# Last stage: three column groups in work in a turn, transposes a step ahead, TensorE in program order

## The chip, the cores and the metric

The kernel runs on one core of a Trainium2 chip. The metric is the time of one execution on that core in microseconds (us). TensorE (PE in the profile) does matrix products and transposes and writes to PSUM; PEld is its weight loading; VectorE is DVE, ScalarE is ACT, GpSimd is POOL, SyncE is SP. Everything here is float32.

## What is computed

Two layers follow each other on an image x of 4 x 64 x 256 x 256. The change touches only the end of the second layer: attention along columns, and the feed-forward network after it. Cut to that, the reference is (E = 64 channels, 4 heads, one query and one key number per head):

```python
h = h + _lin_attn(_ln(h.swapaxes(1, 2), cn_g, cn_b), col_wq, ..., col_bo).swapaxes(1, 2)
f = _ln(h, fn_g, fn_b)
f = gelu(f @ w1.T + b1) @ w2.T + b2          # 64 -> 256 -> 64
return moveaxis(h + f, -1, 1)                # back to channels first

def _lin_attn(x, ...):                       # per column, over its 256 rows
    q = elu(x @ wq.T + bq) + 1;  k = elu(x @ wk.T + bk) + 1;  v = x @ wv.T + bv
    q = q / mean(q);  k = k / sum(k)
    return (q @ (k.T @ v)) @ wo.T + bo
```

## The kernel before

The kernel is a chain of stages with DRAM tensors between them. `stage_d`, the last, reads `hd` (the image after the row attention, rows outermost, 64 channels innermost) and writes the output. Its unit is a **column group**: one image b and 32 columns, so 4 x 8 = 32 groups. A group's tile `h` holds 128 x 32 x 2 x 64 numbers: partition = row within a half, then column, row half, channel (16 KB a partition). `load` fetches it with four DMAs from SP's queue.

A group passes through two generators, which the loop at the end of the stage advances in alternation with `_steps`, one piece of each per round:

- `attn` takes the sums of the layer norm (`spread`, four times 128 x 1024 elements: sum, centring, square, sum of squares), transposes `h` in eight steps of four 128 x 128 blocks (L1203), copies each result out of PSUM on ScalarE (L1205), and forms the query and key numbers (L1212). After the last step it scales them (`rstd`, L1219, L1220), puts them through elu (`feature`, L695 and L696) and has `f` and `kz` (L1229, L1232). Then comes a serial part: key-value sums (L1238, L1242), a transpose (L1245, L1259), `mix` (L702 to L710), and the result, added to `h` in place (L1271 and L1274 on TensorE, L1277 on VectorE). At last the layer norm of the new `h` (`spread`, `rstd`) fills the tiles `xf` (L1288), of which there are five.
- `ffn` takes the previous group in eight steps. In each step r it turns `xf` (four transposes at L1298, copied to `xfT` at L1300), multiplies by w1 (four products of 64 rows each, L1311; each pair uses the two halves of the array's rows) with Gelu on ScalarE (L1313), and then gathers in one PSUM bank the transposed `h` (L1319) plus the products with w2 (four, 64 columns wide, L1322). VectorE adds the bias and writes to the output tile `st` (L1324). The transposes of step r + 1 stand behind the w1 products of step r.

So two groups are in work in a turn of the loop: attention of group n, feed-forward of group n - 1, and 33 turns in all. Group n is loaded one turn ahead; three `h` tiles exist. Two groups share one `st` of 128 x 128 x 64, and after every second group eight DMAs from POOL's queue write it to the output: 512 KB each, in runs of 64 columns (256 bytes).

PSUM has eight banks: six for tiles called `mm`, two for `sm`. Every product above of 512 columns takes one `mm`.

What sets the order on an engine is a planner: it takes the instructions as the program issues them, and orders each engine's own list by readiness in its model of time, earlier-issued ones first. So in this kernel an engine's list is not the program's order, TensorE's included; each engine then runs its list strictly in order, waiting where an operand or a buffer isn't ready.

Of the kernel before, what the change touches and what calls it, by code (L numbers as in the profile page):

```python
# [249 lines left out]
def kernel(ctx: ExitStack, tc: tile.TileContext, x, packs, fd, out, off):  # L250
# [888 lines left out]
    def stage_d():  # L1139
        with ExitStack() as cs:  # L1140
# [27 lines left out]
            def load(b, g):  # L1168
                h = p.tile([128, 32, 2, C], F32, name="h", bufs=3)
                for rh in (0, 1):  # L1170
                    for j in (0, 1):
                        SY.dma_start(h[:, 16 * j:16 * j + 16, rh, :], hd[b, rh * 128:(rh + 1) * 128, :, 2 * g + j, :])
                return h

            def spread(src, n, s2):

                s1 = p.tile([128, n], F32, tag="ln_s", name="ln_s")
                V.tensor_reduce(s1, src, AX.X, ALU.add)  # L1178
                xc = p.tile([128, n, C], F32, tag="xc", name="xc")
                V.scalar_tensor_tensor(xc, bc(s1, C), -LN_S, src, ALU.mult, ALU.add)  # L1180
                sq = p.tile([128, n, C], F32, tag="ln_sq", name="ln_sq")
                S.activation(sq, xc, AF.Square)  # L1182
                V.tensor_reduce(s2, sq, AX.X, ALU.add)  # L1183
                return xc

            def rstd(s2, n):
                s3 = p.tile([128, n], F32, tag="ln_d", name="ln_d")
                S.activation(s3, s2, AF.Sqrt, bias=eps_t, scale=LN_S)
# [4 lines left out]
            def attn(h, xfs):  # L1193

                qp = p1.tile([128, 32, 32], F32, name="qp")
                v1 = p1.tile([128, 64], F32, name="v1")
                for r in range(8):
                    if r % 2 == 0:
                        k = r // 2
                        spread(h[:, 8 * k:8 * k + 8].rearrange("p c a e -> p (c a) e"), 16, v1[:, 16 * k:16 * k + 16])  # L1200
# [5 lines left out]
                    yield  # L1206
                    if r % 4 == 0:
                        qk = sm()
# [5 lines left out]
                    if r % 4 == 3:  # L1214

                        V.transpose(qp[:, r // 4 * 16:r // 4 * 16 + 16].rearrange("p c m -> p (c m)"), qk)
# [4 lines left out]
                yield  # L1221
# [8 lines left out]
                fv = f.rearrange("p r k c h -> p r k (c h)")  # L1230
                kz = p1.tile([128, 2, 128], F32, name="kz")
                V.tensor_tensor(kz.rearrange("p r (c h) -> p r c h", h=4), f[:, :, 1], rs.rearrange("p (c r) -> p r c", r=2).unsqueeze(3).to_broadcast([128, 2, 32, 4]), ALU.mult)  # L1232
                yield

                t = mm()
                for rh in (0, 1):
                    for g in range(4):
                        T.matmul(t[g * 32:(g + 1) * 32, :], kz[:, rh, g * 32:(g + 1) * 32], h[:, 8 * g:8 * g + 8, rh, :], start=(rh == 0), stop=(rh == 1))  # L1238
                qs = sm()
# [39 lines left out]
                for hf in (0, 1):  # L1279
                    v2 = p.tile([128, 32], F32, name="v2")  # L1280
                    xcs = []
                    for k in (2 * hf, 2 * hf + 1):
                        xcs.append(spread(h[:, 8 * k:8 * k + 8].rearrange("p c a e -> p (c a) e"), 16, v2[:, (k % 2) * 16:(k % 2) * 16 + 16]))
                        yield
                    rs = rstd(v2, 32)
                    for k in (0, 1):
                        xf = p.tile([128, 8, 2, C], F32, name="xf", bufs=5)
                        V.tensor_tensor(xf.rearrange("p c a e -> p (c a) e"), xcs[k], bc(rs[:, k * 16:k * 16 + 16], C), ALU.mult)  # L1288
                        xfs.append(xf)

            def ffn(h, xfs, st, gi):


                def first(r):
                    t = mm()
                    xf = xfs[r // 2]
                    for i in range(4):
                        T.transpose(t[:, i * 128:(i + 1) * 128], xf[:, (r % 2) * 4 + i].rearrange("p a e -> p (a e)"), ident)  # L1298
                    xT = p.tile([128, 512], F32, name="xfT")
                    S.copy(xT, t)  # L1300
                    return xT

                yield
# [66 lines left out]
```

## Time and profile before

| | us |
|---|---|
| median of three runs | 8939.46 (8939.42 to 8940.79) |
| the profiled execution | 8937.15 |
| its span, first to last instruction | 8935.4 |
| within it: the stage's first transpose of `h` (L1203) | 6690.1 |
| first w1 product (L1311) | 6742.5 |
| first w1 product of the last turn | 8863.2 |
| last write to `st` ends | 8908.3 |

The span less than the time by 1.75 us is launch and end. The stage has its start (52.4 us), 31 like turns ((8863.2 - 6742.5) / 31 = 68.4 us each), a last turn with the feed-forward network alone (45.1 us), and the output's last DMAs (27.1 us): 2245.3 us, a quarter of the span. Whole-kernel shares (PE 92%, DVE 66%, ACT 51%, POOL 13%) are means over stages with other limits, and say little of this one; a stretch of one turn is to be read on its own. DMAs take 29% of the 16 engines' time in this stage: 15.3% are the output's, 14.1% the loads of `h`.

### The profile page before, as it was taken

The page shows a single profiled execution, that of the slowest core. Times are in us where ns is not written, and L with a number is a line of the kernel's source. Part 1 is how long each engine was busy: PE and PEld are TensorE (multiplying, and loading weights), DVE is VectorE, ACT ScalarE, POOL GpSimd, SP SyncE. Part 2 cuts the span into 40 slices and gives each one's busy share as a digit, 9 for nine tenths or more (in the row PEclk, how much of TensorE's full clock was granted, in tenths as well). Part 3 has the DMA queues.
Part 4 walks back from the last instruction along what each step waited for, and adds up shares of the span by engine and source line. Part 5 has one row for each costly group of instructions (what it writes and reads, how often), then busy time and mean ns, then how long its engine had stood idle before and what let it go on. Part 6 is the DMA issues. An engine that isn't in the chain of part 4 may idle for free. (4 is left out here: it accounts for less than half of the span.)

```text
span 8935.4 us, 143218 instructions
## 1 busy us (share of the span) xinstructions
PE 8237.0 (92%) x57518; PEld 4221.3 (47%) x57518; DVE 5940.4 (66%) x8506; ACT 4587.6 (51%) x7782; POOL 1133.1 (13%) x1828
## 2 busy tenths in 40 slices
PE   8999999699999998999999999999988888989897
PEld 6777777344444443333333344444443333333333
DVE  7766666377777773222222488888877888788776
ACT  4455554455555552222222366666656677667765
POOL 1111111112222221000000011111110000000000
PEclk9999999799999999999999999999998999999998
DMA  7777777799999998888888755555542233233232
GB/s 164 160 187 184 183 185 176 219 357 390 392 390 389 394 378 304 299 296 297 298 298 295 240 170 170 170 170 170 169 121 45 54 70 67 48 76 65 50 67 48
DMA packets 1258502, 1832.48 MB, mean 205 GB/s; under 512 B 335600, under 2 KB 1040112, under 8 KB 1196656
## 3 DMA queue, kind: packets, MB, share of 16 engines
q1 hardware_dynamic: 1053296, 1034.63, 38.5%
q0 software_dynamic: 204544, 788.69, 27.0%
q8 instruction: 456, 7.47, 0.3%
q14 instruction: 206, 1.69, 0.1%
HBM read 967.65 MB, written 788.53 MB: 197 GB/s over the span
## 5 line engine op out<-in xcount | busy, mean ns | idle before, releaser
L915 DVE TENSOR_TENSOR y<-ge,mm 128x512 f32<-128x512 f32 (+1 forms) x640 | 406.0, 634 | 1211.8 <-ACT ge L914 1211.8
L882 PE MATMUL mm<-t,w 128*128 128x512 f32 (+1 forms) x2560 | 1093.7, 566 | 19.1 <-DMA t<-td 19.1
L914 ACT ACTIVATE ge<-mm 128x512 f32<-128x512 f32 (+1 forms) x640 | 354.7, 554 | 1253.8 <-PE mm L889 1253.8
L1313 ACT ACTIVATE hg<-mm,b 128x512 f32<-128x512 f32 x1024 | 631.7, 685 | 331.0 <-PE mm L1311 328.7
L775 PE MATMUL mm<-gp,wc 128*64 128x510 f32 (+1 forms) x3072 | 702.4, 596 | 89.0 <-DVE xm L785 51.0
L620 PEld LDWEIGHTS mm<-wqk,gp 128*128 128x128 f32 x6144 | 728.0, 197 | 99.0 <-issue 60.7
L620 PE MATMUL mm<-wqk,gp 128*128 128x128 f32 x6144 | 761.5, 282 | 1.1 <-POOL gp L589 0.9
L882 PEld LDWEIGHTS mm<-t,w 128*128 128x128 f32 x2560 | 455.2, 189 | 647.5 <-issue 436.9
L1322 PE MATMUL mm<-hg,pack_d 128*64 128x512 f32 x2048 | 579.8, 609 | 101.0 <-ACT hg L1313 101.0
L1311 PE MATMUL mm<-xfT,w 64*128 64x512 f32 x2048 | 637.7, 665 | 2.9 <-ACT xfT L1300 2.2
L830 ACT COPY tb<-mm 128x512 f32<-128x512 f32 x512 | 300.1, 587 | 631.3 <-PE mm L824 631.2
L889 PE MATMUL mm<-t,w 64*64 64x504 f32 (+1 forms) x5120 | 575.6, 555 | 0.0
L824 PE MATMUL mm<-xl,pack_c 64*128 64x512 f32 x2048 | 511.7, 601 | 6.0 <-ACT xl L812 4.6
L775 PEld LDWEIGHTS mm<-gp,wc 128*64 128x64 f32 x3072 | 277.9, 137 | 468.8 <-issue 330.8
L316 ACT ACTIVATE ln_sq<-xn 128x1024 f32<-128x1024 f32 x256 | 274.2, 1071 | 365.9 <-DVE xn L314 365.8
L318 DVE TENSOR_REDUCE ln_v<-ln_sq 128x16 f32<-128x1024 f32 x256 | 312.0, 1219 | 184.2 <-ACT ln_sq L316 184.1
L1324 DVE TENSOR_SCALAR st<-mm,pack_d 128x512 f32<-128x512 f32 x256 | 279.2, 1090 | 171.8 <-PE mm L1322 171.8
L970 PE MATMUL mm<-ya,pack_e 128*64 128x512 f32 x1024 | 381.7, 616 | 11.4 <-DMA ya<-yd 11.4
L1182 ACT ACTIVATE ln_sq<-xc 128x1024 f32<-128x1024 f32 x256 | 266.9, 1055 | 219.8 <-DVE xc L1180 219.7
L828 DVE COPY tb<-mm 128x512 f32<-128x512 f32 x512 | 344.8, 685 | 23.7 <-PE mm L824 18.2
L1311 PEld LDWEIGHTS mm<-xfT,w 64*128 64x128 f32 x2048 | 220.5, 202 | 271.5 <-issue 159.4
L889 PEld LDWEIGHTS mm<-t,w 64*64 64x64 f32 x5120 | 158.1, 132 | 374.4 <-issue 374.4
(458 smaller groups left out, 15178.4 us busy)
## 6 DMA issues: line engine op xcount, KB each, us to landing
t<-td SPq DMA_DIRECT2D x256, 1152.0 KB, 10.0
td<-tb POOLq DMA_DIRECT2D x144, 1024.0 KB, 16.1
td<-tb POOLq DMA_DIRECT2D x288, 512.0 KB, 13.9
yd<-y POOLq DMA_DIRECT2D x128, 1152.0 KB, 10.1
ya<-yd SPq DMA_DIRECT2D x192, 512.0 KB, 5.7
xs<-in_x_dram SPq DMA_DIRECT2D x128, 512.0 KB, 6.8
projd<-pj POOLq DMA_DIRECT2D x256, 256.0 KB, 6.1
gp<-projd SPq DMA_DIRECT2D x128, 512.0 KB, 9.3
```

Of the source, the lines that this page charges most:

```text
L620: T.matmul(qp[:, k * 128:(k + 1) * 128], gp[:, 2 * i + k // 2, at + dx:at + dx + 128], wqk[:, dx, :], start=(dx == 0), stop=(dx == 2))
L775: T.matmul(tv[i * 64:(i + 1) * 64, :, o], wc[2 * pr + i][:, dx, :], gps[i][:, 2 * r:2 * r + 2, i_], start=(dx == 1), stop=False, skip_grou ...
L824: T.matmul(t, inT[q, hf * 128:(hf + 1) * 128], xls[b // 2, s][q, :, 2 * y:2 * y + 2].rearrange("p f y t -> p f (y t)"), start=True, stop=True)
L828: V.tensor_copy(o, i_)
L882: T.matmul(t[:, :n], w[:, 0:128], x_[:, c, :], start=True, stop=False, skip_group_check=True)
L889: T.matmul(t[po:po + 64, :n].rearrange("p (n c) -> p n c", c=64)[:, :, o], w[q:q + 64, 128:192], x_[q:q + 64, c, i_], start=False, stop=Tr ...
L914: S.activation(ge[:, :n], ts[0][k][:, :n], AF.Gelu)
L915: V.tensor_tensor(y[:, c, :].rearrange("p n c -> p (n c)"), ge[:, :n], ts[1][k][:, :n], ALU.mult)
L970: T.matmul(t[b * 64:(b + 1) * 64, :], owT, ya[:, :, 2 * r:2 * r + 2, b * 64:(b + 1) * 64].rearrange("p f y t -> p y f t"), start=True, sto ...
L1311: T.matmul(t, w1[rh * 64:(rh + 1) * 64, i * 128:(i + 1) * 128], xT[rh * 64:(rh + 1) * 64], start=True, stop=True)
L1313: S.activation(g, t, AF.Gelu, bias=b1[:, i:i + 1])
L1322: T.matmul(y[rh * 64:(rh + 1) * 64, :], w2[:, i, :], hg[i * 2 + rh], start=False, stop=(i == 1), skip_group_check=True)
```

## The change

- **Three groups.** `attn` is cut in two. `scores(n + 1)` does the sums, transposes and query/key numbers up to `f` and `kz`; `result(n)` does the serial part, the addition to `h`, and `xf`. The feed-forward network of group n - 1 runs beside both. A group so takes three turns, and the loop 34. `h` is loaded two turns ahead, into four tiles; `xf` has six.
- **Transposes a step ahead.** The network is cut in three functions. In step i of a turn the program issues the transposes of step i + 2 (`turn`), the w1 products and Gelus of step i + 1 (`first`), a piece of `scores` and a piece of `result`, then the residual and w2 products of step i (`second`), and again a piece of each. This runs on across the border between groups: step i counts over all groups.
- **Order.** All of it stands in a block in which TensorE's instructions are issued in the program's order. The other engines keep the planner.
- `spread` takes two blocks in one call: both sums, centrings and squares first, then both sums of squares. `scores` issues its four blocks in two such calls.
- `st` becomes 128 x 128 x 32, one for each group, with four DMAs of 512 KB for each; runs of 32 columns (128 bytes).

The arithmetic is the same. The diff, with most of the removed lines cut (the functions before stand above):

```diff
@@ -1166,59 +1166,86 @@
...
             def load(b, g):
-                h = p.tile([128, 32, 2, C], F32, name="h", bufs=3)
+                h = p.tile([128, 32, 2, C], F32, name="h", bufs=4)
                 for rh in (0, 1):
                     for j in (0, 1):
                         SY.dma_start(h[:, 16 * j:16 * j + 16, rh, :], hd[b, rh * 128:(rh + 1) * 128, :, 2 * g + j, :])
                 return h
 
...
+            def spread(h, ks, v):
+                xcs, sqs = [], []
+                for k in ks:
+                    src = h[:, 8 * k:8 * k + 8].rearrange("p c a e -> p (c a) e")
+                    s1 = p.tile([128, 16], F32, tag="ln_s", name="ln_s")
+                    V.tensor_reduce(s1, src, AX.X, ALU.add)
+                    xc = p.tile([128, 16, C], F32, tag="xc", name="xc")
+                    V.scalar_tensor_tensor(xc, bc(s1, C), -LN_S, src, ALU.mult, ALU.add)
+                    sq = p.tile([128, 16, C], F32, tag="ln_sq", name="ln_sq")
+                    S.activation(sq, xc, AF.Square)
+                    xcs.append(xc)
+                    sqs.append(sq)
+                for i, k in enumerate(ks):
+                    V.tensor_reduce(v[:, 16 * i:16 * i + 16], sqs[i], AX.X, ALU.add)
+                return xcs
...
-            def attn(h, xfs):
+            def scores(n):
+                h = hs[n]
                 qp = p1.tile([128, 32, 32], F32, name="qp")
                 v1 = p1.tile([128, 64], F32, name="v1")
...
+                def up(r):
                     t = mm()
                     for i in range(4):
                         T.transpose(t[:, i * 128:(i + 1) * 128], h[:, r * 4 + i].rearrange("p a e -> p (a e)"), ident)
                     xT = p.tile([128, 512], F32, name="xT")
                     S.copy(xT, t)
...
+                    return xT
+                def score(r, xT, qk):
...
                     for g in range(4):
                         T.matmul(qk[g * 32:(g + 1) * 32, r % 4 * 128:r % 4 * 128 + 128], cwt, xT.rearrange("p (c n) -> p c n", c=4)[:, :, g * 32:(g + 1) * 32],
                                  start=True, stop=True)
...
+                def back(k, qk):
+                    V.transpose(qp[:, k * 16:k * 16 + 16].rearrange("p c m -> p (c m)"), qk)
+                xT = up(0)
+                spread(h, (0, 1), v1[:, 0:32])
+                yield
+                yield
+                qk = sm()
+                for r in range(7):
+                    if r == 4:
+                        back(0, qk)
+                        qk = sm()
+                    score(r, xT, qk)
+                    xT = up(r + 1)
+                    yield
+                    if r < 5:
+                        if r == 4:
+                            spread(h, (2, 3), v1[:, 32:64])
+                        yield
+                score(7, xT, qk)
+                back(1, qk)
                 rs = rstd(v1, 64)
...
-                yield
...
@@ -1227,15 +1254,20 @@
...
-                fv = f.rearrange("p r k c h -> p r k (c h)")
                 kz = p1.tile([128, 2, 128], F32, name="kz")
                 V.tensor_tensor(kz.rearrange("p r (c h) -> p r c h", h=4), f[:, :, 1], rs.rearrange("p (c r) -> p r c", r=2).unsqueeze(3).to_broadcast([128, 2, 32, 4]), ALU.mult)
+                fks[n] = f, kz
+            def result(n):
+                h = hs[n]
+                f, kz = fks.pop(n)
                 yield
 
...
+                fv = f.rearrange("p r k c h -> p r k (c h)")
...
@@ -1278,73 +1310,82 @@
                     yield
                 for hf in (0, 1):
                     v2 = p.tile([128, 32], F32, name="v2")
-                    xcs = []
-                    for k in (2 * hf, 2 * hf + 1):
-                        xcs.append(spread(h[:, 8 * k:8 * k + 8].rearrange("p c a e -> p (c a) e"), 16, v2[:, (k % 2) * 16:(k % 2) * 16 + 16]))
-                        yield
+                    xcs = spread(h, (2 * hf, 2 * hf + 1), v2)
+                    yield
                     rs = rstd(v2, 32)
                     for k in (0, 1):
-                        xf = p.tile([128, 8, 2, C], F32, name="xf", bufs=5)
+                        xf = p.tile([128, 8, 2, C], F32, name="xf", bufs=6)
                         V.tensor_tensor(xf.rearrange("p c a e -> p (c a) e"), xcs[k], bc(rs[:, k * 16:k * 16 + 16], C), ALU.mult)
-                        xfs.append(xf)
...
+                        xfs[n, 2 * hf + k] = xf
                     yield
...
+            def turn(i):
+                n, r = divmod(i, 8)
+                t = mm()
+                xf = xfs[n, r // 2]
+                for k in range(4):
+                    T.transpose(t[:, k * 128:(k + 1) * 128], xf[:, (r % 2) * 4 + k].rearrange("p a e -> p (a e)"), ident)
+                xT = p.tile([128, 512], F32, name="xfT")
+                S.copy(xT, t)
+                xTs[i] = xT
+            def first(i):
+                xT = xTs.pop(i)
+                hgs[i] = []
+                for k in (0, 1):
+                    for rh in (0, 1):
+                        t = mm()
+                        T.matmul(t, w1[rh * 64:(rh + 1) * 64, k * 128:(k + 1) * 128], xT[rh * 64:(rh + 1) * 64], start=True, stop=True)
+                        g = p.tile([128, 512], F32, tag=f"hg{rh}{k}", name=f"hg{rh}{k}")
+                        S.activation(g, t, AF.Gelu, bias=b1[:, k:k + 1])
+                        hgs[i].append(g)
+            def second(i):
+                n, r = divmod(i, 8)
+                h, hg = hs[n], hgs.pop(i)
+                if r == 0:
+                    sts[n] = p.tile([128, 128, 32], F32, name="st")
+                st = sts[n]
+                y = mm()
+                for k in range(4):
+                    T.matmul(y[:, k * 128:(k + 1) * 128], h[:, r * 4 + k].rearrange("p a e -> p (a e)"), ident, is_transpose=True, start=(k == 0), stop=False, skip_group_check=True)
+                for k in (0, 1):
+                    for rh in (0, 1):
+                        T.matmul(y[rh * 64:(rh + 1) * 64, :], w2[:, k, :], hg[k * 2 + rh], start=False, stop=(k == 1), skip_group_check=True)
+                V.tensor_scalar(st[:, :, 4 * r:4 * r + 4].rearrange("p r c -> p c r"), y.rearrange("p (c r) -> p c r", c=4), K("b2"), None, ALU.add)
+                if r == 7:
+                    b, g = seq[n]
+                    for q in (0, 1):
                         for rh in (0, 1):
...
+                            y0 = rh * 128 + q * 64
+                            G.dma_start(out[b, :, y0:y0 + 64, g * 32:g * 32 + 32], sts[n][rh * 64:(rh + 1) * 64, q * 64:(q + 1) * 64])
+                    del hs[n]
 
             seq = [(b, g) for b in range(B) for g in range(8)]
...
+            N = len(seq)
+            hs, fks, xfs, xTs, hgs, sts = {}, {}, {}, {}, {}, {}
+            hs[0] = load(*seq[0])
+            with tc.manual_schedule(engines={mybir.EngineType.PE}):
+                for n in range(-1, N + 1):
+                    if 0 <= n + 2 < N:
+                        hs[n + 2] = load(*seq[n + 2])
+                    gs = scores(n + 1) if n + 1 < N else iter(())
+                    gr = result(n) if 0 <= n < N else iter(())
+                    for r in range(8):
+                        i = 8 * (n - 1) + r
+                        if 0 <= i + 2 < 8 * N:
+                            turn(i + 2)
+                        if 0 <= i + 1 < 8 * N:
+                            first(i + 1)
+                        next(gs, 0)
+                        next(gr, 0)
+                        if 0 <= i < 8 * N:
+                            second(i)
+                        next(gs, 0)
+                        next(gr, 0)
+                    _steps(gs, gr)
 
     stage_d()
 
```

## The prediction

> **What bounds it now.** I first cut the stage into turns by the repeats of the L1311 group and asked for the busy times of one turn (columns: stretch, length, then busy time and instructions of each engine, granted TensorE clock, DMA share, GB/s):
>
> ```profile
> 7221.44:7289.72 68.28, 60.87 (x350) 26.64 (x350) 54.53 (x68) 47.38 (x70) 2.57 (x4) 0.97 0.15 34
> ```
>
> No engine is full: TensorE 60.87 us (89%), VectorE 54.53 (80%), ScalarE 47.38. So I read TensorE's timeline of that turn, with what ended each wait:
>
> ```profile
> 7221.44 3.39 PE L1311 MATMUL mm<-xfT,w 64*128 64x512 f32 x8 [0.18 <-ACT xfT L1300]
> ...
> 7229.50 1.98 PE L1311 MATMUL mm<-xfT,w 64*128 64x512 f32 x6
> 7231.41 0.42 PE L1212 MATMUL sm<-xT,cwt 128*32 128x128 f32 x8
> 7231.77 1.12 PE L1311 MATMUL mm<-xfT,w 64*128 64x512 f32 x2
> ...
> 7247.70 1.07 PE L1322 MATMUL mm<-hg,pack_d 128*64 128x512 f32 x2
> 7250.32 2.23 PE L1322 MATMUL mm<-hg,pack_d 128*64 128x512 f32 x6 [1.55 <-ACT hg L1313]
> ...
> 7279.91 2.81 PE L1322 MATMUL mm<-hg,pack_d 128*64 128x512 f32 x8 [1.63 <-ACT hg L1313]
> ...
> 7288.33 0.66 PE L1298 MATMUL mm<-pack_k,xf 128*128 128x128 f32 x4 [3.32 <-DVE xf L1288]
> ```
>
> Three things are to be seen. The border between groups costs a wait of 3.32 us for `xf`, which VectorE has only just made. Gelus come late for L1322 twice. And after the border's wait the eight L1311 instructions take 3.39 us; elsewhere they take 1.92. Also, where the planner put L1212 inside a set of L1311 (7229.50 to 7232.82), the set took 1.91 + 1.05 us: a pair that would use both row halves was broken up. The waits that the timeline names in this turn sum to 3.32 + 1.63 + 1.55 + 0.37 + 0.32 + 0.18 + 0.17 = 7.5 us.
>
> The last turn has only the network, undisturbed, and shows what a step costs:
>
> ```profile
> 8878.43 1.99 PE L1311 MATMUL mm<-xfT,w 64*128 64x512 f32 x8
> 8880.35 0.66 PE L1298 MATMUL mm<-pack_k,xf 128*128 128x128 f32 x4
> 8880.84 0.60 PE L1319 MATMUL mm<-pack_k,h 128*128 128x128 f32 x4
> 8881.37 1.94 PE L1322 MATMUL mm<-hg,pack_d 128*64 128x512 f32 x8
> 8883.24 1.99 PE L1311 MATMUL mm<-xfT,w 64*128 64x512 f32 x8
> ```
>
> From start to start that is 1.92 + 0.49 + 0.53 + 1.87 = 4.81 us. By starts in the same way, `scores` costs 0.59 (L1203) + 0.36 (L1212) = 0.95 a step, and `result` 1.85 (L1238) + 0.92 (L1242) + 0.25 (L1245) + 0.26 (L1259) + 0.43 (L702) + 3.90 (L1271, L1274, twice) = 7.6 a turn. TensorE's own work in a turn: 8 x 4.81 + 8 x 0.95 + 7.6 = **53.7 us**. A turn is 68.3, so 14.6 us are lost: 7.5 in waits, and some 7 in slow or broken sets (border 1.5, two broken pairs 2.1, late Gelus 1.4 and 0.9, the rest small).
>
> Here a rule is to be weighed. Read as a floor, the row's 60.87 us of busy PE would leave at most 7.4 us a turn, and with the waits below (7.2) nothing at all. The Trainium skill (Perfetto Trace Analysis, Identifying the Most-Contended Engine) says that matmul occupancy is a bad measure of distance from the roofline, and to read weight loading as well: 26.64 / 68.28 = 39%. I go by the starts, 53.7, since the undisturbed step shows it at work.
>
> **The change, part by part.**
>
> *Transposes a step ahead, across the border.* `xf` of the next group is made at r = 3 and 4 of a turn and first turned at r = 6, two steps (over 11 us) later. The 3.32 us wait goes, with it the slow set after it (1.5 us). Gelus get a whole step instead of half of one before L1322 wants them, which covers a table load, square-root work and table load back (1.28 + 0.35 + 1.28 = 2.9 us between Gelus): the 1.55 and 1.63 go, and their drawn-out sets.
>
> *Program order.* The four products of `first` stand together, so no pair is broken: -2.1 us. All removals together lead to the 53.7. In exchange TensorE can no longer take other ready work when it must wait. Three places do:
>
> 1. `kz`. The last L1212 of a group is followed, before L1238 wants `kz`, by `second` (2.40), `turn` (0.49), `first` (1.92), `up` (0.59) and `second` (2.40): 7.8 us. Before, VectorE's rows from there run
>
> ```profile
> 7246.59 0.71 DVE L1216 STREAM_TRANSPOSE qp<-sm 128x512 f32<-128x512 f32 x1
> ...
> 7248.30 0.55 DVE L1190 RECIPROCAL ln_r<-ln_d 128x64 f32<-128x64 f32 x1 [1.01 <-ACT ln_d L1188]
> ...
> 7254.81 0.42 DVE L1232 TENSOR_TENSOR kz<-f,ln_r 128x256 f32<-128x256 f32 x1
> ```
>
> and L1212 had ended at 7244.8, so `kz` came 10.4 us after it. 10.4 - 7.8 = 2.6 us of wait. Behind L1238 stand L1242, L1245 and all of the next step, and ScalarE's Gelus wait for those. Ends: 0 (the chain's own operations sum to about 6) and 11 (rival below); I take 2.6, the row's latency.
>
> 2. The two L1271 blocks take four of the six `mm` banks at once. The first stands about 1 us behind `first`, whose four Gelus take 2.4 us: 1.4 us of wait. The second needs the four additions of the first (2.48 us, L1277) and stands a `second` (2.40) behind it, plus the `st` write of 1.09: 1.2. Sum 2.6; ends 0 (before, these rows show no wait named) and 5.
>
> 3. VectorE's load is uneven. At r = 3 it has 2 x (1.21 + 1.22 + 1.20) = 7.26 for `spread`, 1.09 for `st`, 0.35 and 2.36 for `xf`: 11.1 us, and r = 4 the same, while TensorE has 4.81 + 0.95 = 5.8. With six banks TensorE gets about a step ahead of the `st` writes, not more. Ends: 0, if VectorE does `scores`' sums early, in r = 1 and 2 (3.3 and 6.1 us of its work against 6.5 and 9.7 of TensorE's; `h` has landed a turn before), and 10.6, if `st` stands behind both `spread`s. I take 2, nearer the low end, because VectorE in the turn before does run `spread` in its free places.
>
> 53.7 + 2.6 + 2.6 + 2 = **61 us a turn** (60.9).
>
> *Three groups, four `h`.* The same instructions per group, so no busy time is added. SP's four loads of a group are issued a turn earlier; they take 5.4 us to land and now have a turn and more. If that cover were gone they would cost the 5.4 once per group; SP has nothing else in its queue.
>
> *Activation tables.* Still three square roots and one exponential a group between Gelus, 8 loads of 1.28 us; one or two may merge or be added (±2.6 us of ScalarE, which has 47.4 of 61): nothing.
>
> *`st`, one per group.* L1324 takes 1.09 us with an inner stride of 256 bytes, L1277 of the same size 0.68; the stride becomes 128. Ends: -3.3 us a turn of VectorE and 0; I take 0. POOL issues four DMAs a group as before, 1.10 us each for 2048 runs; 4096 runs may take 2.2, 8.8 us a turn on an engine that has 2.6 busy. The only other POOL work, the memset of `zn`, is done a turn early.
>
> The runs are halved to 128 bytes. Row: at the end eight DMAs with 8 x 2048 runs of 256 bytes take 23.5 us, 27.1 from the last `st` write to the end of the span. Four DMAs with 4096 runs are as many runs. By the run that stays 27.1; by the byte it is 15. The Trainium skill (DMA: Bandwidth & Descriptors, Specifications) speaks against it: under 512 bytes the DMA does a read-modify-write. If that doubled a run's time, the end would be near 50. But 256 bytes are under 512 already, so the row holds that price: I take 25. In a turn the output's share was 15.3%; by the run it becomes 34% of 61 us, with the loads' 16% half of the DMA engines' time, hidden behind the turn. Without that cover (a st tile comes round after two turns) it would cost what exceeds a turn, and there is none.
>
> **The sum.** Start: `scores` of group 0 alone until `kz`, 6690.1 to 6711.2 = 21 us, then a turn of `result(0)` with `scores(1)`; `result` alone took 41 (to 6752.2), and VectorE's second load makes it 47: 68, where 52.4 were. Then 30 turns of 61 = 1830; one without `scores`, 61 - 7.6 and a little less VectorE: 52; the last, 8 x 4.81 = 38.5; end 25. Together 2013.5 against 2245.3: -232 us. 8937.15 - 232 = **8705**. The profiled execution stands 2.3 us under the median, well inside what is uncertain here.
>
> **Rivals.**
>
> - *VectorE becomes the bound.* Its 54.5 us of a turn, plus about 2.5 of the serial part that nothing fills (before: waits for L1274, L1238, L702 of 3.3 + 2.1 + 1.9): 57 us a turn. 68 + 1710 + 48 + 38.5 + 25 = 1889.5: **8581**. For it: 54.5 and 53.7 are nearly equal. Against it: it asks 95% of an engine that runs in list order.
> - *PSUM and ScalarE hold TensorE oftener.* Every step takes seven `mm` of six; at r = 7 ScalarE has Gelus, square root, exponential and three table loads, 7.8 us against TensorE's 5.2. With item 3 at half its upper end (5.3), and 1 and 2 at 6 together: 65 us. 68 + 1950 + 56 + 38.5 + 25 = 2137.5: **8829**.
> - *Slower: steps in lockstep.* If each `st` write stands behind all of its step's `spread`, TensorE in program order waits in each step for the slowest engine: 10.6 + 6.5 + 9.7 + 11.1 + 11.1 + 9.1 + 6.7 + 7.8 = 72.6 us a turn, total 2373, **9065**. It decides from 68.5 us a turn (where 31 turns and the longer start eat all). For it: nothing else can fill TensorE's waits now. Against it: `spread`'s inputs are ready early, and the list is planned with TensorE's order known.
> - *Nothing told apart*, turns between 68 and 69: the 14.6 us lost are replaced by as many.
>
> **Chances.** Forecast (59 to 63 us a turn, 8643 to 8767) 50%; VectorE's bound 15%; PSUM and ScalarE (63 to 68) 25%; lockstep 7%; nothing 3%. Under 0.2%, 18 us, a measurement of this kernel hardly tells a change. So faster 90%, same 3%, slower 7%. The range goes to 8590, which leaves out half of the VectorE case, and to 8850, which leaves out lockstep, nothing, and the top of the third case.
>
> **What would show it.** Right: turns of about 61 us between the first L1311 of each eighth step; L1298 without a wait for `xf`; L1311 always x8 in 1.92; granted clock near 1.00 in the stage; waits at L1238 for `kz` of some 2.6 us. Wrong: waits at L1311 or L1319 for the bank of a `st` write or a Gelu of more than 5 us a turn (third or lockstep case); VectorE over 92% busy (first rival); an end after the last `st` write well over 27 us (the runs). The forecast falls if L1238's wait is over 5 us, or the start over 90.

## The result, and the profile after

The changed kernel takes 8836.58 us (median of 4 runs, 8829.69 to 8839.12). Its ratio to the kernel before is 0.9885, with a 95% interval of 0.9867 to 0.9902: faster, by some 100 us where 232 were forecast. The time lies inside the range on record (8590 to 8850), but near its upper end. The profiled execution took 8839.12 us, with a span of 8837.3, and is compared here with the profiled 8937.15 of before.

The forecast was a sum over pieces of the stage. The same pieces, cut in the trace of after:

| piece | forecast, us | trace of after, us | from where to where |
|---|---|---|---|
| start | 68 | 71.3 | 6688.05 to 6759.34, the first transposes of turn 1 |
| 30 turns | 1830 | 1968.4 | to 8727.74 |
| turn without `scores` | 52 | 53.3 | to 8781.00 |
| last turn | 38.5 | 37.8 | to 8818.79, the last `st` write |
| end | 25 | 18.5 | to 8837.3 |
| sum | 2013.5 | 2149.3 | 2245.3 before |

The sum is 136 us too low, and the thirty turns alone are 138 too low. The first of them took 78.3 us (6759.34 to 6837.61), with a wait of 10.07 us for `kz` and half the clock behind it. The other 29 are the rule, (8727.74 - 6837.61) / 29 = 65.2 us each, where 61 were forecast. (From L1269 to L1269 the mean is 65.0, since the last such turn is short, as will be seen.) So the question is what fills a turn.

Two turns of after, from one L1269 to the next, in busy times (the columns are those of the same view before: stretch, length, busy time and instructions of PE, PEld, DVE, ACT, POOL, granted clock, DMA share, GB/s):

```profile
7240.16:7304.55 64.39, 58.14 (x349) 26.42 (x350) 53.58 (x67) 47.66 (x70) 6.63 (x5) 1.00 0.33 65
6912.35:6981.17 68.82, 62.58 (x350) 28.43 (x351) 53.56 (x67) 47.67 (x70) 6.63 (x5) 0.93 0.31 62
```

As before, no engine is full: TensorE is busy for 90% of the first turn, VectorE for 83%. TensorE's timeline of the first turn, cut to the places where it loses time and one set that is undisturbed (start, length, instructions, and in brackets the wait before it with what ended it). L1339 are the w1 products and L1356 those with w2, L1210 and L1353 transposes of `h`, L1306 the result that is added to `h`; in the kernels of e1 and later most of these lines stand four or five further down.

```profile
7240.16 1.92 PE L1269 MATMUL mm<-h,kz 128*32 128x512 f32 x16 [3.04 <-DVE kz L1258]
...
7260.00 1.36 PE L1339 MATMUL mm<-xfT,w 64*128 64x512 f32 x4
7262.10 1.72 PE L1339 MATMUL mm<-xfT,w 64*128 64x512 f32 x4 [0.73 <-DVE h L1309]
...
7267.58 1.99 PE L1339 MATMUL mm<-xfT,w 64*128 64x512 f32 x8
...
7273.33 3.02 PE L1339 MATMUL mm<-xfT,w 64*128 64x512 f32 x8
...
7282.92 0.66 PE L1210 MATMUL mm<-pack_k,h 128*128 128x128 f32 x4 [0.46 <-ACT xfT L1330]
7284.25 0.66 PE L1353 MATMUL mm<-pack_k,h 128*128 128x128 f32 x4 [0.68 <-DVE st L1357]
```

The border between groups has no wait for `xf` any more. L1356, which used to stand 1.55 and 1.63 us for late Gelus, comes as x8 in 1.94 us without a wait. What is left is one wait of 3.04 us for `kz`, short waits, and four sets of L1339 that take longer than the undisturbed 1.92 from start to start. What makes `kz` late is to be seen on VectorE. Its timeline at the beginning of the same turn:

```profile
7242.15 0.69 DVE L1281 TENSOR_TENSOR zm<-mm,pack_d 128x512 f32<-128x512 f32 x1 [2.13 <-PE mm L1269]
...
7246.79 0.29 DVE L1293 COPY zT<-mm 65x128 f32<-65x128 f32 x1 [2.15 <-PE mm L1291]
7249.11 1.11 DVE L1357 TENSOR_SCALAR st<-mm,pack_d 128x512 f32<-128x512 f32 x1 [2.03 <-PE mm L1356]
...
7254.94 2.48 DVE L1309 TENSOR_TENSOR h<-mm,h 128x512 f32<-128x512 f32 x4 [3.11 <-PE mm L1306]
...
7295.74 0.52 DVE L1196 RECIPROCAL ln_r<-ln_d 128x64 f32<-128x64 f32 x1
7296.17 1.17 DVE L1183 SCALAR_TENSOR_TENSOR xc<-ln_s,h 128x1024 f32<-128x1024 f32 x1
...
7299.37 1.20 DVE L1189 TENSOR_REDUCE v<-ln_sq 128x16 f32<-128x1024 f32 x1
...
7304.00 0.40 DVE L1258 TENSOR_TENSOR kz<-f,ln_r 128x256 f32<-128x256 f32 x1
```

While `result` runs its serial part, VectorE has nothing to do: four waits of 2 to 3 us are shown, and all of them make 64.39 - 53.58 = 10.8 us. Then, from 7259.5 to `kz`, there is not one gap. And within that full stretch stands work that is not wanted yet. The `ln_r` of 64 columns at 7295.74 already belongs to this group's scores, so the `xc` and `v` behind it are sums of the *next* group: its `spread` over quarters 0 and 1, six operations of about 1.2 us. The planner, which goes by readiness, put them ahead of `kz`. The last group of all has no next group, so no such sums stand ahead of its `kz`. There L1269 comes without a wait, and the turn before it took 59.56 us:

```profile
8733.28 1.92 PE L1269 MATMUL mm<-h,kz 128*32 128x512 f32 x16
```

The chain of waits says the same for the turn before (start, length, what):

```profile
7195.14 0.68 DVE h L1309
...
7239.76 0.27 DVE kz L1258
7240.03 0.14 issue
7240.16 1.02 PE mm L1269 x5
```

Between 7195.14 and 7240.03 every step of the chain is VectorE's or an issue: 44.9 us of a turn in which TensorE's own waits don't lengthen the turn. The other 19.5 us are TensorE's and the serial part's.

### The profile page after: what moved, and what is told of

Read it like the earlier page. It is cut to its first block, busy times and chain, and to the rows that moved or that the text cites. A ratio compares the mean times of both kernels' runs of the same rounds, so it can differ in the third digit from the quotient of the medians.

```text
span 8837.3 us, 143300 instructions
## 1 busy us (share of the span) xinstructions
PE 8179.4 (93%) x57518; PEld 4220.4 (48%) x57518; DVE 5910.0 (67%) x8506; ACT 4597.1 (52%) x7781; POOL 1205.3 (14%) x1828
## 4 chain that ended last, share of the span: by engine, by line
PE 51%; DVE 31%; ACT 12%; issue 4%; DMA 2%; POOL 0%; SPq 0%; DVEq 0%; ACTq 0%; POOLq 0%
PE mm L882 12%; PE mm L889 6%; PE mm L775 4%; PE mm L620 4%; DVE ln_s L1181 3%; DVE v L1189 3%; PE mm L824 3%; DVE xc L1183 3%; ACT xl L812 2%; ACT ln_sq L316 2%; PE mm L970 2%; DVE st L1357 2%; DVE xn L314 2%; PE mm L1339 2%; DVE h L1121 2%
## 5 line engine op out<-in xcount | busy, mean ns | idle before, releaser
L882 PE MATMUL mm<-t,w 128*128 128x512 f32 (+1 forms) x2560 | 1094.6, 566 | 18.4 <-DMA t<-td 18.4
L1339 PE MATMUL mm<-xfT,w 64*128 64x512 f32 x2048 | 627.8, 631 | 25.0 <-DVE h L1309 22.6
L1356 PE MATMUL mm<-hg,pack_d 128*64 128x512 f32 x2048 | 496.8, 606 | 0.0
L1363 POOL DMA_DIRECT2D out_dram<-st x128 | 209.1, 1638 | 1723.1 <-DVE st L1357 1640.9
L1339 PEld LDWEIGHTS mm<-xfT,w 64*128 64x128 f32 x2048 | 227.1, 188 | 257.4 <-issue 113.2
```

The lines of the kernel that those rows point to most:

```text
L882: T.matmul(t[:, :n], w[:, 0:128], x_[:, c, :], start=True, stop=False, skip_group_check=True)
L1339: T.matmul(t, w1[rh * 64:(rh + 1) * 64, k * 128:(k + 1) * 128], xT[rh * 64:(rh + 1) * 64], start=True, stop=True)
L1356: T.matmul(y[rh * 64:(rh + 1) * 64, :], w2[:, k, :], hg[k * 2 + rh], start=False, stop=(k == 1), skip_group_check=True)
```

## The experiments

Three theories were set against one another. **A**: VectorE's list sets the turn, since sums of the next group were hoisted ahead of `kz` and leave VectorE idle in the serial part. **B**: the six `mm` banks and ScalarE's table loads and Gelus hold TensorE. **C**: TensorE's fixed order does, since nothing may fill its waits. Each ratio below is to the kernel before, with its 95% interval. "Of after" and "of e1" say to which kernel a diff applies.

### e1: the hoisted sums queued behind `zn` (of after)

```diff
                 xT = up(0)
-                spread(h, (0, 1), v1[:, 0:32])
                 yield
                 yield
+                if n == 0:
+                    spread(h, (0, 1), v1[:, 0:32])
+                else:
+                    with tc.issue_after(zni[0].ins):
+                        spread(h, (0, 1), v1[:, 0:32])
...
-                V.tensor_scalar(zn[:, 0:64], z, rz, None, ALU.mult)
+                zni[0] = V.tensor_scalar(zn[:, 0:64], z, rz, None, ALU.mult)
```

> One edit to the changed kernel: the first two blocks of the next group's layer-norm sums are queued on VectorE behind the zn of the group in its serial part, so they can't stand ahead of kz. Theory A (VectorE's list sets the turn: 45 us without a gap from the additions to h up to kz, then 10.7 us idle in the serial part): these 7.3 us move from the gapless part into the idle places, the wait of L1269 for kz goes under 1 us, a turn goes from 65.0 to 58-61 us, the time to 8640-8740 us. Theory B (six PSUM banks and ScalarE's Gelus hold TensorE): the slow w1 sets stay, a turn stays at 64-66 us, the time at 8810-8850. Theory C (TensorE's fixed order is what costs): as B.

Measured: 8728.06 us, ratio 0.9767 (0.9753 to 0.9782). That is some 110 us below after. A turn, in the same columns as above, and TensorE at its beginning:

```profile
7211.95:7273.33 61.38, 58.08 (x352) 26.45 (x350) 54.04 (x67) 47.83 (x71) 6.63 (x6) 1.00 0.33 68
```

```profile
7210.08 1.94 PE L1360 MATMUL mm<-hg,pack_d 128*64 128x512 f32 x8
7211.95 1.92 PE L1273 MATMUL mm<-h,kz 128*32 128x512 f32 x16
```

The same work now takes 61.38 us, and the products with `kz` follow without a wait. VectorE's timeline shows where the six operations have gone:

```profile
7216.16 0.26 DVE L1292 TENSOR_SCALAR zn<-z,rz 128x64 f32<-128x64 f32 x1
7216.33 2.34 DVE L1181 TENSOR_REDUCE ln_s<-h 128x16 f32<-128x1024 f32 x2
7218.58 2.35 DVE L1183 SCALAR_TENSOR_TENSOR xc<-ln_s,h 128x1024 f32<-128x1024 f32 x2
...
7221.05 2.33 DVE L1189 TENSOR_REDUCE v<-ln_sq 128x16 f32<-128x1024 f32 x2
```

They fill the places where VectorE waited 2.15 and 2.03 us before. This is A: not less work, only another place in one engine's list. The chain of a turn in e1 is TensorE's for the most part, so VectorE's list no longer sets it alone.

### e8: the same sums queued directly behind `kz` (of after)

```diff
                 xT = up(0)
-                spread(h, (0, 1), v1[:, 0:32])
+                if kzi:
+                    with tc.issue_after(kzi[0].ins):
+                        spread(h, (0, 1), v1[:, 0:32])
...
-                V.tensor_tensor(kz.rearrange("p r (c h) -> p r c h", h=4), f[:, :, 1], rs.rearrange("p (c r) -> p r c", r=2).unsqueeze(3).to_broadcast([128, 2, 32, 4]), ALU.mult)
+                kzi[0] = V.tensor_tensor(kz.rearrange("p r (c h) -> p r c h", h=4), f[:, :, 1], rs.rearrange("p (c r) -> p r c", r=2).unsqueeze(3).to_broadcast([128, 2, 32, 4]), ALU.mult)
```

> As the run with the sums behind zn, but they are queued on VectorE only behind kz. So kz comes as early as there, but 7.3 us of sums may stand ahead of zm, and the serial part waits for those. Theory A as it stands now (what costs is that VectorE has no work of its own to do in the serial part): between the two, 62-65 us a turn, the time 8740-8840, with L1269 no longer waiting for kz and the transpose of zn waiting 2 us or more. If the wait for kz (3.0 us) alone were the cost: 61-62 us, the time 8715-8745.

Measured: 8811.42 us, ratio 0.9860 (0.9845 to 0.9875), turns of 64.5 us, some of 62.9. TensorE's waits over 7000 to 8600 us (engine and line, what it waited for, us in total, times, longest):

```profile
PE mm L1295 <- DVE zn L1292: 45.6, 25, 2.2
...
```

No row for `kz` is left, and yet little is won: the sums now stand ahead of `zm` and `zn`, and TensorE waits for `zn`, 45.6 / 25 = 1.8 us a turn. In the turns of 64.5 us the granted clock falls behind that wait (0.66 over 7235 to 7240), and L1360 takes 3.09 us there instead of 1.94; the turns of 62.9 are spared that. So the 3.1 us over e1's turn are the wait and its clock. Removing the named wait is not enough. What counts is that the sums lie in VectorE's idle places behind `zn`.

### e2: the square root left out of the row statistics (of after)

```diff
-                S.activation(s3, v, AF.Sqrt, bias=eps_t, scale=LN_S)
+                S.activation(s3, v, AF.Identity, bias=eps_t, scale=LN_S)
```

> The changed kernel with Identity in place of the square root in the last stage's rstd (the square root is left out, so the output is another): no table is loaded for it and back, which takes some 6 x 1.28 = 7.7 us of ScalarE out of each turn. Theory A: only the chain before kz gets shorter, a turn is 62.5-65 us, the time 8760-8840. Theory B: TensorE gets its banks back sooner in the steps where they were late, a turn is 58-61 us, the time 8640-8720. Theory C: no change, 65.

Measured: 8832.96 us, ratio 0.9888 (0.9873 to 0.9903), so no change from after, although six of the eight table loads a group are for the square root or for the way back. The waits moved: that for `kz` went from 72.9 us in 24 to 49.9 in 25, and those for `xT` and `xfT` rose to 51.1 and 46.8. VectorE's stretch still stands on the chain, from 7252.34 to 7290.24 of one turn without a step of TensorE or ScalarE. So the table loads are not what the 65.2 us are made of, which is what A expected and B did not (C expected no change either). They do hold TensorE at some places, as e7 shows more clearly.

### e3 and e4: TensorE's fixed order alone

e3 takes the fixed order out of the changed kernel; e4 puts it into the kernel before.

```diff
-            with tc.manual_schedule(engines={mybir.EngineType.PE}):
+            with ExitStack():
                 for n in range(-1, N + 1):
```

```diff
             st = None
+            with tc.manual_schedule(engines={mybir.EngineType.PE}):
-            for n in range(len(seq) + 1):
+                for n in range(len(seq) + 1):
```

> The changed kernel without the block that fixes TensorE's order: the planner orders TensorE too. Theory A: VectorE's list is nearly the same, so the turn is set as before, 64-67 us, the time 8810-8900. Theory B: 64-67 too. Theory C: TensorE's waits (3 us for kz, 2.5 for banks) are filled with other work, a turn is 58-62 us, the time 8640-8750.

> The kernel before with one edit: TensorE's instructions of the last stage in the program's order, two groups as they were. Theory A and B: the wait for xf at the border stays (3.3 us), the late Gelus stay or grow (they have half a step), broken pairs are gone (-2.1 us), a turn is 66-72 us, the time 8880-9060. Theory C: TensorE waits where it filled before, a turn is over 72 us. If the fixed order alone brings what the change brought, a turn is 65 us, the time 8840.

Measured: e3 8823.05 us, ratio 0.9872 (0.9856 to 0.9888), 64.9 us a turn; e4 9009.37, ratio 1.0083 (1.0068 to 1.0098), 70.6 us a turn. Without the fixed order the changed kernel is as fast as with it, and the fixed order by itself costs the kernel before some 70 us. The gain of the change therefore comes from its other parts together (the three groups, the transposes a step ahead and the output written once per group were not tried apart); the program's order on TensorE brings nothing measurable. So C falls; A and B, which expected the same of e3, are not told apart by it. TensorE fills its time otherwise in e3, with waits of 1.1 us for `f` in place of those for `kz`, but VectorE idles in the same places (its waits over 7000 to 8600 us, in the columns of e8's):

```profile
DVE h L1309 <- PE mm L1306: 94.0, 48, 3.1
...
DVE zm L1281 <- PE mm L1269: 74.2, 24, 3.2
```

That is 2.0 and 3.1 us at a time, in the serial part again. VectorE is idle there whatever order TensorE has.

### e5: e1 without the fixed order

The edit is that of e3, made to e1.

> The sums queued behind zn, and TensorE ordered by the planner again. Theory A: VectorE's list is freed in both, and TensorE's order matters little: a turn within 1 us of the 61.4 of the run with the sums behind zn, the time 8700-8760. Theory C (the fixed order costs, or brings, something of its own): more than 2 us a turn off, the time under 8665 or over 8790.

Measured: 8722.43 us, ratio 0.9760 (0.9743 to 0.9776), 61.41 us a turn: as e1. It has the lowest median of all that were run, 216 us below before and 114 below after, though e1 and e11 lie within its interval.

### e7: e1 without the square root

The edit is that of e2, made to e1.

> The sums queued behind zn, and Identity in place of the square root (the square root is left out, so the output is another), which takes some 7.7 us of table loads out of a turn of ScalarE. Theory A, carried on: 60.5-61.5 us a turn, the time 8700-8735. Theory B for what is left: the slow w1 sets (three a turn, together 2.7 us over) go, 57.5-59.5 us a turn, the time 8610-8675.

Measured: 8725.84 us, ratio 0.9764 (0.9749 to 0.9778), turns of 61.07 and 62.67. In e1's chain of a turn ScalarE's square root, table load and Gelus stand between TensorE's steps:

```profile
7253.60 0.72 issue
...
7255.14 1.28 ACT L1345
...
7257.02 1.83 ACT hg L1345 x3
...
7259.38 0.42 PE sm L1219 x8
```

From 7253.6 to 7259.4 the turn waits for ScalarE. It was natural to take these loads for the next bound, and they are in part what holds TensorE: three of the four sets of w1 products that are slow in e1 take their 1.91 us without the loads. But ScalarE's list, which the planner made anew, now has the copies to `xT` and `xfT` behind squares that wait for VectorE. TensorE's and ScalarE's timelines of e7 and, last, one set of e1 for comparison:

```profile
7244.91 1.99 PE L1343 MATMUL mm<-xfT,w 64*128 64x512 f32 x8
...
7249.11 0.66 PE L1210 MATMUL mm<-pack_k,h 128*128 128x128 f32 x4 [1.86 <-ACT xfT L1334]
...
7250.65 3.18 PE L1360 MATMUL mm<-hg,pack_d 128*64 128x512 f32 x8
```

```profile
7247.53 1.06 ACT L1185 ACTIVATE ln_sq<-xc 128x1024 f32<-128x1024 f32 x1 [2.83 <-DVE xc L1183]
7248.49 0.57 ACT L1334 COPY xfT<-mm 128x512 f32<-128x512 f32 x1
```

```profile
7245.59 3.07 PE L1343 MATMUL mm<-xfT,w 64*128 64x512 f32 x8
```

The waits for `xT` and `xfT` rise to 42.2 and 48.6 us in 26 each (9.2 and 10.4 in e1), TensorE runs at half its clock behind some of them, and nothing is won. A step on the chain is not a price: what was taken away came back at another place, by another list.

### e6: the multiplication that makes `xf`, on GpSimd (of e1)

```diff
-                        V.tensor_tensor(xf.rearrange("p c a e -> p (c a) e"), xcs[k], bc(rs[:, k * 16:k * 16 + 16], C), ALU.mult)
+                        G.tensor_tensor(xf.rearrange("p c a e -> p (c a) e"), xcs[k], bc(rs[:, k * 16:k * 16 + 16], C), ALU.mult)
```

> The sums queued behind zn, and the four multiplications that make xf on GpSimd (an operation of that size there took 1.97 us in the trace, 1.22 on VectorE). VectorE has 4.9 us less in a turn. Theory A, carried on (VectorE's list still sets the 61.4 us): a turn is 57-59.5 us, the time 8600-8680. Theory B (what is left over 53.7 is late banks, from ScalarE's Gelus behind table loads and squares): 60.5-61.5 us, the time 8705-8735.

Measured: 8925.59 us, ratio 0.9988 (0.9979 to 0.9996), 68.0 us a turn. This met no theory's expectation. VectorE was to be freed of 4 x 1.2 us a turn; its timeline shows what it got:

```profile
7429.36 0.30 DVE L1196 RECIPROCAL ln_r<-ln_d 128x32 f32<-128x32 f32 x1
7431.68 4.04 DVE L1183 SCALAR_TENSOR_TENSOR xc<-ln_s,h 128x1024 f32<-128x1024 f32 x2 [2.02 <-POOL xf L1322]
```

The next `xc` waits 2.02 us for GpSimd, because the buffers of `xc` come round after two and GpSimd reads them for 3.76 us a pair; and then two of it take 4.04 us instead of 2.35. ScalarE's squares are late in turn, and TensorE waits up to 5.0 us for `xT`. All but some 13 us of e1's gain is given back. So e6 does not show what a lighter VectorE would bring; it was not tried with four buffers of `xc`.

### e9, e10 and e11: the rest of the turn

In e1 L1343 still waits 0.73 us for an addition to `h`, in a set that takes 3.7 us from start to start; an `ln_s` of `spread` stands between the first addition and the other three. e9 puts `spread` behind all four; e10 also gives `xc` four buffers; e11 is e5 with four buffers of `xc`.

```diff
-                        V.tensor_tensor(hh, ts[g].rearrange("p (c e) -> p c e", c=8), hh, ALU.add)
+                        zni[1] = V.tensor_tensor(hh, ts[g].rearrange("p (c e) -> p c e", c=8), hh, ALU.add)
...
-                    xcs = spread(h, (2 * hf, 2 * hf + 1), v2)
+                    with tc.issue_after(zni[1].ins):
+                        xcs = spread(h, (2 * hf, 2 * hf + 1), v2)
```

```diff
-                    xc = p.tile([128, 16, C], F32, tag="xc", name="xc")
+                    xc = p.tile([128, 16, C], F32, tag="xc", name="xc", bufs=4)
```

> The sums queued behind zn, and result's own sums queued behind the last of the eight additions to h (a sum stood among the last four, and the w1 set behind it waited 0.73 us for a bank and took 3.1 us in two parts instead of 1.92). Theory A with banks as the next limit at this place: a turn loses 0.8-1.5 us, 59.9-60.6, the time 8680-8710. If VectorE's list alone decides: 61.4, 8720-8735.

> As the run with the additions first, with four tiles for the centred blocks (xc) instead of two, so that VectorE can centre the next blocks while the last wait for their square roots. If VectorE's waits for its own tiles are part of what is left: 58.5-60 us a turn, the time 8630-8690. If not (TensorE, with banks and Gelus, holds the turn now): within 0.5 us of the run with the additions first.

> The sums queued behind zn, TensorE ordered by the planner, and four tiles for the centred blocks (the last run that had four was 18 us faster than the one without, both with the additions first). If VectorE's waits for its own tiles are part of what is left of the 61.4 us: 60-61 us a turn, the time 8675-8715. If the gain was one of that order only: 61-62, the time 8710-8745.

Measured: e9 8772.79 us, ratio 0.9816 (0.9799 to 0.9832), 62.8 us a turn; e10 8754.88, ratio 0.9797 (0.9782 to 0.9812), 62.27 us; e11 8726.99, ratio 0.9765 (0.9752 to 0.9778), 61.6 us. e9 did remove what it aimed at, and lost time, which neither of its expectations had. TensorE's timeline has the set in one piece, and further on a new wait; its waits over 7000 to 8600 us show where the time came back:

```profile
7245.57 2.56 PE L1344 MATMUL mm<-xfT,w 64*128 64x512 f32 x8
...
7263.50 0.78 PE L1358 MATMUL mm<-pack_k,h 128*128 128x128 f32 x4 [1.53 <-DVE st L1362]
7264.21 3.46 PE L1361 MATMUL mm<-hg,pack_d 128*64 128x512 f32 x8
```

```profile
PE sm L1219 <- ACT xT L1212: 51.6, 26, 2.2
PE mm L1358 <- DVE st L1362: 39.9, 26, 1.5
```

Everything behind the additions starts later on VectorE, so ScalarE's squares and the `st` writes do too: 2.0 us a turn for `xT` (e1: 0.35) and 1.5 for the bank of an `st` write (0.67). Four buffers probably give a little of that back: the intervals of e9 and e10 overlap, but all four runs of e10 (8752.1 to 8756.8 us) lie below all four of e9 (8768.5 to 8774.7) on the same chip. e11 gains nothing over e5.

## Why the gain was less than half of the forecast

**What held.** The wait of 3.32 us for `xf` went, the late Gelus before the w2 products went, broken pairs of L1339 are gone. A step with `scores` and no disturbance takes 7272.75 - 7266.99 = 5.76 us, exactly the 4.81 + 0.95 of the forecast, so the 53.7 us of TensorE's own work stand. The busy time of PE, 60.87 us a turn before, was no floor: it is 58.1 now. The turn without `scores` and the last one came within 1.3 us. Measured, a turn stands like this:

| part of a turn, us | forecast | after | e1 |
|---|---|---|---|
| TensorE's own work | 53.7 | 53.7 | 53.7 |
| wait for `kz` | 2.6 | 3.1 | 0 |
| half clock behind that wait, mean | 0 | 0.8 | 0 |
| banks and uneven VectorE | 4.6 | 7.6 | 7.7 |
| turn | 61 | 65.2 | 61.4 |

The third row is the mean turn less the undisturbed one (65.2 - 64.4), the fourth what is left.

**The step that failed is in item 3 of the forecast**, where VectorE "does `scores`' sums early, in r = 1 and 2", and 2 us are taken "because VectorE in the turn before does run `spread` in its free places". In after it does not. It has done the first half of those sums already, ahead of `kz`, and idles in r = 0 to 2. The argument took a habit of the old list for one of the new list, which the planner makes anew. So VectorE's gapless stretch sets the turn, a path that the sum over TensorE's waits doesn't have. e1's edit moves nothing but these sums and takes 65.2 - 61.4 = 3.8 us off a turn, of the 4.3 that were missed (60.9 was the unrounded sum).

**Two more terms were wrong, and nearly cancel.** The wait for `kz` was taken for latency of a chain, 10.4 us against 7.8 of cover, which no order could mend. e1 mends it without touching the chain, so with the sums in the free places it is 0 and not 2.6; the 3.1 of after have another reason. And the allowance for banks was too small: items 2 and 3 have 2.6 + 2, where 7.6 were lost in after and 7.7 in e1. In the turn of after shown above I find 7.0 of them: waits of 0.46 + 0.68 + 0.36 + 0.30 + 0.68 = 2.5, and slow sets of L1339, beyond 1.91 each, of 1.84 + 1.04 + 0.96 + 0.66 = 4.5. In e1's turn it is again 7.0 (2.6 in waits, 4.4 in slow sets), all but 0.4 at the same places, so the place of the sums is not what makes this term. By what ended the waits, the additions to `h` cost 1.8 (item 2 said 2.6), banks of `st` writes 1.4, and ScalarE 3.8, of which the forecast says "nothing" under its activation tables. It weighed their share of ScalarE's time, and not the moment at which they come: in the set at 7273.33 the Gelus that free the banks stand behind a square root and its two table loads.

```profile
7270.51 1.28 ACT L1194 ACT_TABLE_LOAD   x1
...
7273.44 1.27 ACT L1341 ACTIVATE hg<-mm,b 128x512 f32<-128x512 f32 x2
```

A slow set shows no wait of its own, because it is the weight load (PEld) in the middle of it that waits. Over 7000 to 8600 us, first after, then e7, which has no square root (there the largest of these waits for ScalarE, where e1 has 38.7 and 22.1 us):

```profile
PEld mm L1339 <- ACT hg L1341: 41.3, 98, 0.6
PEld mm L1339 <- ACT xT L1212: 21.1, 50, 0.7
```

```profile
PEld mm L1343 <- ACT xT L1212: 1.4, 6, 0.2
...
```

So what holds these sets is shown; what they cost is not, since the time came back elsewhere in e7. That e1 reaches the forecast 61 us, with 0 in place of 2.6 and 7.7 in place of 4.6, is partly luck.

**The rivals.** "PSUM and ScalarE hold TensorE oftener" has the right time, 8829, and late banks of about its size (item 3 at 5.3, where 7.6 - 1.8 = 5.8 were lost), but not the cause of the miss: e2 takes three quarters of the table loads away and gains nothing, and e1 gains 110 us without touching banks or ScalarE. "VectorE becomes the bound" gave 8581. It names the engine, but what counted was the order of VectorE's list and not its load: e1 has the same busy time (53.58 and 54.04 us) in a shorter turn. It also allowed 2.5 us of idle time where the three waits that it lists sum to 7.3; e1 has 61.4 - 54.0 = 7.4, after has 10.8. "Lockstep" did not come about: the longest of TensorE's waits in the steady turns is that for `kz`.

**The end was better than forecast.** I took 25 us, between 15 by the byte and 27.1 by the run. It is 18.5. POOL's last issues and the DMA queues over 7000 to 8380 us (queue: packets, MB, share of 16 engines):

```profile
8826.62 1.64 POOL L1363 DMA_DIRECT2D out_dram<-st  x1 [2.53 <-issue]
```

```profile
q0 software_dynamic: 12096, 44.05, 18.4%
...
out_dram<-st POOLq DMA_DIRECT2D x84, 512.0 KB, 9.1
```

With runs of 128 bytes instead of 256, the output's share in a turn is 18.4% (15.3% before, and 34% was forecast by the run), and a DMA lands 9.1 us after its issue (12.2). Per group, estimated from these shares and turns, that is 0.184 x 65.2 = 12.0 us of the DMA engines against 0.153 x 68.4 = 10.5, so the price goes with the bytes and only a little with the runs. POOL's issue went from 1.10 us to 1.64 for twice the runs, not to 2.2. (The forecast read POOL's 2.6 us off a turn that holds only part of a batch of issues; before, the eight of two turns take 8.7.)

**What stays open.** The 7.7 us over 53.7 in e1 and e5. Neither table loads of the square root (e7), nor the place of the additions (e9), nor the buffers of `xc` (e11) gave any of it back when changed one at a time. In e7 VectorE has the chain again, from 7231.09 to 7259.20 of a turn, so the next bound may be VectorE's load or ScalarE's order; neither was tried without a side effect. The exponential's table, and another order of Gelus and banks, were not tried. The waits of 10.62 and 10.07 us for `kz` in the first two groups, at the start, were not worked on either.

## What to carry to other kernels

An engine that is busy for 83% can still set the turn. Look for a long stretch without a gap that ends in what everyone waits for, and for idle time right behind it; then ask which operations in the stretch nobody wants yet, and queue them behind the serial part. Removing the wait itself (e8) is not the same thing, and work moved to another engine (e6) brings costs of its own. And where a change makes a scheduler plan anew, the order that it had in the old trace is no evidence for the order in the new one.

## What the hardware showed that was not expected

**One wait, three prices.** The wait for `kz` is 3.04 or 3.05 us in every turn, but turns take 64.4, 65.8 or 68.8 us. In the longest, TensorE goes on at half its clock:

```profile
6912.35 3.64 PE L1269 MATMUL mm<-h,kz 128*32 128x512 f32 x16 [3.05 <-DVE kz L1258]
```

The same sixteen take 1.92 us at 7240.16, and the granted clock of the two turns is 0.93 and 1.00. That costs 68.82 - 64.38 = 4.4 us more there; the mean over 28 turns was 0.8 us. Shorter waits were enough in other runs: behind 1.86 us in e7 and 1.53 us in e9, both shown above, the w2 products took 3.18 and 3.46 us instead of 1.94, at a granted clock of 0.63 (7249.11 to 7253.76) and 0.58 (7263.5 to 7267.6). The Trainium skill (TensorE: Matmul & The Clock Gate, What's actually happening) says that the clock falls to half after at least one idle window of about 3.4 us, and that the windows run freely. By the figure alone none of these waits would be enough, so here the measurement decides: waits of about half that length can cost as much again. That it is some turns only would fit windows that run freely, which no run here tested.

**GpSimd and VectorE at once.** In e6 the group of L1183 over 7000 to 8600 us took 1643 ns on average, where e1 has 1215, without a change to it. Its durations are (count, then shortest, median and longest in ns, of e6):

```profile
L1183 DVE SCALAR_TENSOR_TENSOR xc<-ln_s,h x189: 1208/1214/2909, 7012.4 to 8599.4; 128x1024 f32<-128x1024 f32 x189
```

In e1 the longest took 1223. In e6 48 of them, one in each pair that runs beside a GpSimd multiplication, take 2.9 us. The Trainium skill (SBUF — State Buffer, Who interferes with whom) says that a VectorE instruction with two operands in SBUF contends with a GpSimd instruction that reads SBUF, which is this case: L1183 reads `h` and `ln_s`. Of the 4.8 us a turn that e6 took off VectorE, two pairs gave 2 x 1.7 = 3.4 back.
